# In the tail of a four-image network: new shares for the convolution and the pooled attention of image 2 beside the linear attention of image 3, whose queued steps leave at two of three taps

## The chip, the cores and the metric

The kernel runs on one core of a Trainium2 chip, in one launch. Its time is the device time of a run in microseconds (us); three runs are shown as median, lowest and highest. Beside them one execution was recorded by the hardware profiler: its span reaches from the first to the last instruction. The engines are PE (matrix multiply, with PEld for its weight loads), DVE (vector), ACT (scalar), POOL (GpSimd) and SP (which issues most DMAs).

## The reference

The input x has shape (4, 256, 64, 64), float32. Four layers follow each other, each on a group-normalised x, and each adds its result to x:

```
x = x + L0(gn(x))   # deformable sampling block with a feed-forward part
x = x + L1(gn(x))   # linear attention
x = x + L2(gn(x))   # 3x3 convolution with binarised weights
x = x + L3(gn(x))   # attention over 2x2 max-pooled keys and values
```

What matters here of L1: a 1x1 product gives q, k and v (768 channels); a 5x5 depthwise convolution of these gives a second set; then

```
vk = einsum(v, k); out = einsum(vk, q) / (einsum(k.sum, q) + eps)
out = relu(bn(conv1x1(out)))
```

L3 has 4096 queries and 1024 pooled keys per image: a softmax over the keys, a weighted sum, and a 1x1 product. The four images are independent of each other.

## The kernel before

Images are processed one behind the other, but the layers of different images overlap. Each layer is a generator: it issues some instructions and yields a cost. `beside(steps, number, *works)` in run() interleaves several of them. A work is a tuple (generator, total, lo, hi); while the share i/number goes from lo to hi, the work is advanced whenever the sum of costs that it has yielded is below total * (share - lo) / (hi - lo). From share hi on it is run to its end, and works whose hi is at most 1 are finished before beside returns; one with hi above 1 keeps a remainder. So the totals and shares set only the order in which instructions are issued. Within ordered() that order is what PE, DVE, ACT and POOL execute; each engine takes its instructions in order and waits where data or a buffer isn't ready.

While the sampling of image 3 runs, it is the long work that others lie beside. After it comes the tail, for which run() sets self.alone and self.spare. In the tail there are three parts:

- The first beside: image 3's feed-forward part (share 0 to 0.27), its linear attention layer1 (0.27 to 1, total LAST), and second(2), which is image 2's convolution layer2 followed by its pooled attention layer3 (0.27 to 1.05, total SECOND).
- The second beside: image 3's convolution, with what is left of image 2's pooled attention (total 150).
- Image 3's pooled attention alone.

In layer1 the channels are worked in three rounds of tile pairs, (2, 4), (3, 5) and then the queries (0, 1), each in 4 chunks of 16 image rows. One depthwise convolution of one tile and chunk has 25 taps. In the tail two of three such sets run on DVE (`depthwise`, L178 and L180, 16 sets or 400 taps in all), the third as products on ACT added up on POOL (`products`, L196 and L200). All that follows a finished set, the transposes and outer products (L873 to L882), relu (L861), and the whole output of a chunk, is put as small steps into the list `later`. A step leaves the list from step(), which is called at each tap:

```
if later and (not alone or count % 2 or not chains):
    todo = later.pop(0)
    todo()
```

In the tail (alone is true) this means at every second tap. `output(c, ...)` puts one chunk's output into the list, as 18 steps: the denominators (L924), their reciprocals (L928, L929), eight times a matmul that spreads a reciprocal over its channels (L937) and the product with the queries on DVE (L941), four projections (L946, four matmuls each, two halves of the chunk with two channel tiles each), relu on ACT (L950), the sum with x (L954), its statistics (L110), and the write (L957). There are four such outputs. What is left in the list after the last tap is taken out by a loop at the end, one step per yield of cost 2; this stretch is called the drain.

layer2 holds all its weights in a 3 MB tile (load at L1037), whose pool is opened after the linear attention's pools are closed, for image 3's convolution on the same side of SBUF. It makes the group norm's scale and offset (L117 to L132, with a Sqrt at L98), loads rows (L1050), normalises them (L1051), transforms them on POOL (L1039), multiplies (L1088, 384 matmuls), and sums into x (L1068 to L1072).

layer3 first makes queries, keys and values (L1145 to L1164). Then it takes 32 tiles of 128 queries: scores (L1188, two matmuls), their maximum (L1189, L1190), Exp (L1194), eight transposes (L1200) and two copies (L1202), the weighted sum (L1206, eight matmuls), its reciprocal (L1209) and scale (L1211). After four tiles come a product (L1216), a scale (L1217), a sum (L1218) and the write (L1219). A tile yields costs of 9.5 in all; a whole pooled attention 376.5, a convolution 191, together SECOND = 568.

Of the kernel before, what the change touches and what calls it, by code (L numbers as in the profile page):

```python
# [18 lines left out]
N, C, H, W = 4, 256, 64, 64  # L19
# [19 lines left out]

CONVOLVE, OFFSETS, BINARY = NB * 9 + 26, 60, 62  # L40
FEED = NB * 40 + 8
LINEAR, LAST = 956, 624
STEPS, BEGUN = 900, 0.22
CONV, SECOND = NB * 22.5 + 11, 568
EPS_BN = 1e-5
EPS_GN = 1e-5
# [25 lines left out]
class Net:  # L72
# [684 lines left out]
    def layer1(self, n, st, st2):  # L757
# [3 lines left out]
        with tc.tile_pool(name=f"la{n}", bufs=1, side="right") as sp, \  # L761
# [10 lines left out]
            ld = sp.tile([P, 4, 2, 32], F32, name="ld")  # L772
            nc.vector.memset(ld, 0.0)

            later, count, aside = [], 0, None
            alone = self.alone
            room = lambda bufs, more=1: bufs + more * alone

            def step(cost, chains=False):


                nonlocal count
                count += chains
                if later and (not alone or count % 2 or not chains):
                    todo = later.pop(0)
                    todo()
                    cost += 0 if alone else getattr(todo, "cost", 0)
                if chains:
                    if count % 8 == 6 if alone else count in LEADS:
                        next(made, None)  # L790
                    if count % 2 and aside:
                        next(aside, None)
                return cost
# [51 lines left out]
            def aggregate(pd, i, name, done, relu=True, **more):  # L845

                acc = self.ps1.tile([P, 16, W], F32, name="agg", tag="agg")
                out = bp.tile([P, 16, W], F32, name=name, tag="ag", bufs=3)
                yield from self.depthwise(acc, pd, self.w5[:, i], 5, 16, W, 0, bias=self.b5[:, i:i + 1],
                                          step=lambda cost: step(cost, True), out=out)  # L850
                end(out, done, relu, **more)

            def products(pd, i, name, done, relu=True, **more):

                out = bp.tile([P, 16, W], F32, name=name, tag="av2", bufs=3)
                yield from self.products(bp, out, pd, self.w5[:, i], 5, 16, W, 0, self.b5[:, i:i + 1], lambda cost: cost)
                end(out, done, relu, **more)
# [54 lines left out]

            def output(c, qp, aq):


                qh = [[q[:, 2 + 8 * h:10 + 8 * h, 2:W + 2] for q in qp] + [v[:, 8 * h:8 * h + 8, :] for v in aq] for h in range(2)]
                rd, pd, xv, ot, pb, pr = [], [], [], {}, {}, {}
                spare = cycle(["mm", "vk"])
# [54 lines left out]
            def chains():  # L973

                for _ in range(3 * NCH):
                    while not ready:
                        next(made)
                        yield None
                    t, tiles, c, pd = ready.pop(0)
                    got = {}  # L980

                    def done(i, v, t=t, c=c, pd=pd, got=got):
                        got[i] = v
                        if len(got) < 2:
                            return
                        if t == 2:
                            return output(c, pd, [got[0], got[1]])
                        outer(t, 1, fl(got[0]), fl(got[1]), False, c == NCH - 1)
                        if c == NCH - 1:
                            later.append(partial(summed, t))  # L990

                    for i, m in enumerate(tiles):
                        more = {} if t == 2 or i else {"accum_out": ks[t][:, 1, c:c + 1]}
                        yield pd[i], m, ("ak", "av")[i], partial(done, i), t == 2 or not i, more

            made, number = rows(), 0
            if alone:
                for _ in range(8):
                    next(made)
                    yield step(0.5)  # L1000
                    yield step(0.5)
            every = chains()

            def chain():

                while not (args := next(every)):
                    yield step(3)
                return args

            while number < 6 * NCH:  # L1010
                count = 0 if not alone and number % 2 == 0 else count
                *args, more = yield from chain()
                if alone:

                    *slow, smore = yield from chain()
                    aside = products(*slow, **smore)
                    yield from aggregate(*args, **more)
                    *args, more = yield from chain()
                    yield from aggregate(*args, **more)
                    for _ in aside:  # L1020
                        pass
                    number += 3
                else:
                    yield from aggregate(*args, **more)
                    number += 1
            while later:
                yield step(2 if alone else 1)


    def layer2(self, n, st, st3, side="left"):  # L1030
# [190 lines left out]
    def run(self):  # L1221
# [5 lines left out]
        feed = lambda n: self.feedforward(n, ssum[n], st[1][n % 2])  # L1227
        linear = lambda n: self.layer1(n, st[1][n % 2], st[2][n % 2])

        conv = lambda n, side="left": self.layer2(n, st[2][n % 2], st[3][n % 2], side)  # L1230
        pooled = lambda n, wide=False: self.layer3(n, st[3][n % 2], wide)

        def second(n):
            yield from conv(n)
            yield from pooled(n)

        def beside(steps, number, *works):


            spent, open_ = [0] * len(works), set(range(len(works)))  # L1240

            def advance(share):
                for j in sorted(open_):
                    work, total, lo, hi = works[j]
                    while j in open_ and lo <= share and spent[j] < total * (share - lo) / (hi - lo) or share >= hi:
                        cost = next(work, None)
                        if cost is None:
                            open_.discard(j)
                        if not cost:
                            break  # L1250
                        spent[j] += cost

            for i, _ in enumerate(steps, 1):
                advance(i / number)
            while any(works[j][3] <= 1 for j in open_):
                advance(1)
# [24 lines left out]
                for n in range(2, N):  # L1281
                    beside(self.sample(n, ssum[n]), rounds, *behind(n - 1), (second(n - 2), SECOND, BEGUN, 1))
        self.idle, self.alone, self.spare = cycle(["acc", "dp"]), True, True
        rest = second(N - 2)
        with ordered():
            beside(range(STEPS), STEPS, (feed(N - 1), FEED, 0, 0.27), (linear(N - 1), LAST, 0.27, 1), (rest, SECOND, 0.27, 1.05))
        self.spare = False
        beside(range(STEPS), STEPS, (conv(N - 1, "right"), CONV, 0, 1), (rest, 150, 0, 1))

        self.banks = cycle(["mm", "mm", "mm", "vk"])  # L1290
        for _ in pooled(N - 1, True):
# [95 lines left out]
```

## Time and profile before

| What | us |
| --- | --- |
| Median of three runs | 7640.25 (7638.07 to 7640.4) |
| Profiled execution, its own time | 7631.35 |
| Its span | 7629.6 |
| Busy in the span: PE, DVE, POOL, ACT | 5886.1, 4810.4, 4936.3, 3530.1 |
| Last matmul of the feed-forward part of image 3 | 6401 |
| Last tap of its linear attention | 7131.7 |
| Last projection (L946) | 7208.4 |
| First and last matmul of its convolution | 7238.2, 7417.1 |

A group of the profile is a line of the kernel with engine, operation and tiles, a count, the busy time and the mean of one in ns, then the engine's idle time just before and what ended it. A matmul in float32 stands as two records of one instruction; a transpose as one. The chain of work that ended last names, from the end back, the instruction that each one waited for, or the one before it on its engine. A busy PE is not always PE at its peak, since the ends of matmuls are modelled. PEclk is the clock that PE was granted, as a share of full speed.

### The profile page before, as it was taken

The numbers are of one execution on the slowest core, as the hardware profiler recorded it, in microseconds if no ns is written. First come the engines' busy times: TensorE is split into PE (matmuls) and PEld (weight loads), VectorE is DVE, ScalarE is ACT, GpSimd is POOL, SyncE is SP. The second block draws the span as 40 slices with busy tenths as digits, with TensorE's granted clock in tenths as the row PEclk, the third lists the DMA queues.
The fourth block names the chain that finished last, engine by engine and source line by source line (L and its number), as shares of the span: only waits on it lengthen the run. The fifth ranks groups of instructions, "written<-read, shape, count | busy, mean of one in ns | idle before, by whom it ended". The sixth has DMA issues, their size and how long they took to land. (4 is left out here: it accounts for less than half of the span.)

```text
span 7629.6 us, 99735 instructions
## 1 busy us (share of the span) xinstructions
PE 5886.1 (77%) x35776; PEld 3454.3 (45%) x35776; DVE 4810.4 (63%) x6045; ACT 3530.1 (46%) x10767; POOL 4936.3 (65%) x4870
## 2 busy tenths in 40 slices
PE   5676666678766677888877778988677789967899
PEld 2333333334433333346644443466444445744487
DVE  6454543633688776228988872279888734999623
ACT  2443433444545443445555544454555523655415
POOL 2777777777777777777777676777776702866210
PEclk7676776779877777999988889999888899988999
DMA  6564655565544444555544445455544432210221
GB/s 185 150 188 140 174 170 145 168 185 164 167 124 131 125 141 135 171 150 154 158 147 138 134 138 175 135 168 156 153 133 140 130 103 71 72 53 34 73 81 51
DMA packets 744383, 1031.75 MB, mean 135 GB/s; under 512 B 354128, under 2 KB 459984, under 8 KB 742352
## 3 DMA queue, kind: packets, MB, share of 16 engines
q0 software_dynamic: 221184, 604.27, 27.4%
q1 hardware_dynamic: 522704, 421.10, 18.6%
q8 instruction: 283, 4.64, 0.3%
q14 instruction: 212, 1.74, 0.1%
HBM read 856.39 MB, written 168.61 MB: 134 GB/s over the span
## 5 line engine op out<-in xcount | busy, mean ns | idle before, releaser
L596 POOL DMA_INDIRECT g<-tab,sl x4608 | 4401.1, 955 | 1715.8 <-issue 1271.0
L178 DVE SCALAR_TENSOR_TENSOR agg<-pad,vec,agg 128x1024 f32<-128x1024 f32 x2280 | 2933.7, 1287 | 64.4
L603 PE MATMUL acc<-g,wm 128*32 128x128 f32 x18432 | 1264.0, 321 | 1161.9 <-ACT at L608 670.8
L588 ACT ACTIVATE wm<-sl,con 128x48 f32<-128x48 f32 x6144 | 1487.8, 365 | 23.6 <-DMA sl<-sd 11.9
L603 PEld LDWEIGHTS acc<-g,wm 128*32 128x32 f32 x18432 | 622.1, 121 | 1836.7 <-ACT at L608 888.3
L1088 PE MATMUL ps<-xd,w 128*128 128x256 f32 x3072 | 721.6, 386 | 8.0 <-DVE x L1072 3.5
L1088 PEld LDWEIGHTS ps<-xd,w 128*128 128x128 f32 x3072 | 579.9, 194 | 116.6 <-issue 35.6
L623 ACT COPY dT<-dp 64x128 f32<-64x128 f32 x1152 | 295.5, 256 | 646.4 <-PE dp L613 379.7
L739 PE MATMUL ps<-x2f,f 128*128 128x512 f32 x1024 | 489.8, 625 | 4.0 <-ACT f L714 4.0
L724 DVE SCALAR_TENSOR_TENSOR hm<-ps,vec,lk 128x512 f32<-128x512 f32 x256 | 191.9, 750 | 466.7 <-ACT lk L741 466.2
L824 PE MATMUL ps<-xr,qw 128*128 128x512 f32 x768 | 461.1, 732 | 13.8 <-ACT pT L1202 5.2
L749 PE MATMUL ps<-hm,f 128*128 128x512 f32 x1024 | 468.0, 604 | 0.0
L1039 POOL TENSOR_TENSOR xd<-xp 128x640 f32<-128x640 f32 x64 | 79.6, 1270 | 514.2 <-ACT xp L1051 416.1
L608 ACT COPY at<-acc 128x256 f32<-128x256 f32 x576 | 214.1, 372 | 423.1 <-PE acc L603 411.2
L741 ACT ACTIVATE lk<-ps,low 128x512 f32<-128x512 f32 x256 | 175.9, 687 | 500.5 <-PE ps L739 498.2
L1206 PEld LDWEIGHTS ps<-gt,pT 128*128 128x128 f32 x2048 | 282.6, 216 | 85.9 <-ACT pT L1202 43.4
L1206 PE MATMUL ps<-gt,pT 128*128 128x129 f32 x2048 | 297.6, 304 | 29.8 <-ACT pT L1202 29.1
L613 PE MATMUL dp<-ident,at 128*128 128x128 f32 x1152 | 265.2, 317 | 65.7 <-ACT dT L623 62.9
L636 PE MATMUL po<-dT,ow 128*128 128x288 f32 x1024 | 297.3, 438 | 21.8 <-ACT dT L631 8.9
L1188 PE MATMUL s<-ph,th 128*128 128x512 f32 x512 | 281.6, 663 | 32.9 <-DVE ot L941 11.0
L200 POOL TENSOR_TENSOR ak<-ak,m 128x1024 f32<-128x1024 f32 x96 | 227.6, 2371 | 117.2 <-ACT m L196 112.8
L727 DVE TENSOR_TENSOR xyf<-xyf,ps 128x512 f32<-128x512 f32 x64 | 44.0, 687 | 402.1 <-PE ps L749 389.3
(243 smaller groups left out, 7565.2 us busy)
## 6 DMA issues: line engine op xcount, KB each, us to landing
g<-tab,sl POOLq DMA_INDIRECT x4608
x<-x SPq DMA_DIRECT2D x128, 512.0 KB
xr<-x SPq DMA_DIRECT2D x96, 512.0 KB
tab<-xo SPq DMA_DIRECT2D x192, 128.0 KB
x<-in_x SPq DMA_DIRECT2D x32, 512.0 KB
y<-yc SPq DMA_DIRECT2D x32, 512.0 KB
yb<-y SPq DMA_DIRECT2D x64, 256.0 KB
x<-yb SPq DMA_DIRECT2D x64, 256.0 KB
```

The source lines that it names most:

```text
L178: nc.vector.scalar_tensor_tensor(to, s, wt, acc, ALU.mult, ALU.add)
L588: nc.scalar.activation(wm[:, :, :, o], blocks[b][:, r:r + WR, G:], AF.Copy, scale=self.con("own")[:, o:o + 1])
L596: nc.gpsimd.indirect_dma_start(out=g[:, i, :], out_offset=None, in_=table, in_offset=bass.IndirectOffsetOnAxis(ap=sl.bitcast(I32)[:, r, i: ...
L603: nc.tensor.matmul(acc[32 * i:32 * i + 32, :], wm[:, r4, 4 * i + 2 * x:4 * i + 2 * x + 2, :], g[:, i, x * P:(x + 1) * P], start=x == 0, st ...
L623: nc.scalar.copy(dT[b][hs, :, r:r + UR], dp[u][hs, :, :, s, :].rearrange("p v g o -> p g v o"))
L636: nc.tensor.matmul(po[m][:, 0:BR * OB], self.ow[:, k, m * P:(m + 1) * P], dT[b][:, k].rearrange("p r o -> p (r o)"), start=k == 0, stop=k ...
L739: nc.tensor.matmul(ps, f1[:, k, m * P:(m + 1) * P], x2[:, k], start=k == 0, stop=k == KT - 1)
L749: nc.tensor.matmul(ps, f2[:, k, m * P:(m + 1) * P], hm[:, k], start=k == 0, stop=k == 4 * KT - 1)
L824: nc.tensor.matmul(ps, qw[:, k, m * P:(m + 1) * P], x[:, k], start=k == 0, stop=k == KT - 1)
L1088: nc.tensor.matmul(ps[:, e], w[:, k, t, 2 * half + e, m * P:(m + 1) * P], v[:, 2 * half + e, k, t:t + 8], start=i % 6 == 0, stop=i % 6 == 5)
L1188: nc.tensor.matmul(s[i], tv[:, 4 * b + j], ph[:, i * 512:(i + 1) * 512], start=True, stop=True)
L1206: nc.tensor.matmul(ps[:, 0:P + 1], pT[:, m], gt[:, m], start=m == 0, stop=m == 7)
```

## The change

- layer1 has a new variable `every`, 2 at first, which takes the place of the 2 in `count % 2`. The first call of output() sets it to 3. With 3, `count % every` is zero at every third tap, so steps leave at two of three.
- The loop that empties the list after the last tap yields 1.2 in the place of 2, and the total LAST is 582 in the place of 624.
- Image 2's convolution and pooled attention are two works of the first beside: the convolution with total 191 from share 0.27 to 0.53, the pooled attention with total 376.5 from 0.53 to 1.02. Before, they were one work with total 568 from 0.27 to 1.05.
- In the second beside the rest of the pooled attention has a total of 60 in the place of 150.

The instructions are the same; their order differs. Line numbers in these texts are those of the kernel before.

```diff
-LINEAR, LAST = 956, 624
+LINEAR, LAST = 956, 582
+CONV2, POOLED = 191, 376.5
...
-            later, count, aside = [], 0, None
+            later, count, aside, every = [], 0, None, 2
...
-                if later and (not alone or count % 2 or not chains):
+                if later and (not alone or count % every or not chains):
...
             def output(c, qp, aq):
 
-
+                nonlocal every
+                every = 3
...
-            every = chains()
+            them = chains()
...
-                while not (args := next(every)):
+                while not (args := next(them)):
...
             while later:
-                yield step(2 if alone else 1)
+                yield step(1.2 if alone else 1)
...
-        rest = second(N - 2)
+        rest = pooled(N - 2)
         with ordered():
-            beside(range(STEPS), STEPS, (feed(N - 1), FEED, 0, 0.27), (linear(N - 1), LAST, 0.27, 1), (rest, SECOND, 0.27, 1.05))
+            beside(range(STEPS), STEPS, (feed(N - 1), FEED, 0, 0.27), (linear(N - 1), LAST, 0.27, 1), (conv(N - 2), CONV2, 0.27, 0.53), (rest, POOLED, 0.53, 1.02))
         self.spare = False
-        beside(range(STEPS), STEPS, (conv(N - 1, "right"), CONV, 0, 1), (rest, 150, 0, 1))
+        beside(range(STEPS), STEPS, (conv(N - 1, "right"), CONV, 0, 1), (rest, 60, 0, 1))
```

## The prediction

> **What bounds the kernel now.** I began with the page's slices, to find where the tail starts and which engine fills it.
>
> ```profile
> PE   5676666678766677888877778988677789967899
> DVE  6454543633688776228988872279888734999623
> POOL 2777777777777777777777676777776702866210
> ```
>
> Each digit is 191 us. POOL's first 0 is the slice from 6104 us, after the gathers: what follows is the tail, and the change touches only that. There DVE has its 9s, then PE. The chain that ended last, cut to the tail, gave me the boundaries, and the busy time by stretch gives the table that everything below is summed from.
>
> ```profile
> core 0: us, PE busy (x) PEld busy (x) DVE busy (x) ACT busy (x) POOL busy (x), PEclk, DMA share, GB/s
> 6401.70:6659.30 257.60, 245.13 (x1140) 194.45 (x1140) 223.28 (x295) 155.91 (x221) 201.71 (x101) 0.97 0.30 87
> 6659.30:7131.70 472.40, 330.48 (x1257) 202.69 (x1256) 442.60 (x500) 263.70 (x368) 292.99 (x124) 0.83 0.13 43
> 7131.70:7208.40 76.70, 73.95 (x268) 40.02 (x268) 31.60 (x54) 22.44 (x37) 0.00 (x0) 0.97 0.14 48
> 7208.40:7238.20 29.80, 21.36 (x98) 15.02 (x97) 12.24 (x35) 14.71 (x23) 1.71 (x2) 0.94 0.66 213
> 7238.20:7417.10 178.90, 176.67 (x825) 154.08 (x823) 50.01 (x107) 20.88 (x27) 38.06 (x31) 0.99 0.27 79
> 7417.10:7629.60 212.50, 193.66 (x1040) 145.98 (x1040) 81.34 (x189) 107.33 (x200) 0.00 (x0) 0.97 0.16 55
> ```
>
> The rows are: the taps of image 3's linear attention up to the 140th of 400, beside image 2's convolution; the other 260 taps, beside image 2's pooled attention; the drain (what the linear attention still has queued after its last tap, up to its last projection, L946); the handoff to image 3's convolution; that convolution; image 3's pooled attention alone. DVE sets the pace of the taps (442.6 of 472.4 us), PE that of the drain (73.95 of 76.7) and of the convolution. In the taps PE has 142 us to spare, afterwards nearly none. So a piece moved from behind the last tap to before it costs its DVE time and gives back its PE time.
>
> The DVE durations come from the groups by line of the taps:
>
> ```profile
> L178 DVE SCALAR_TENSOR_TENSOR agg<-pad,vec,agg 128x1024 f32<-128x1024 f32 x368 | 473.0, 1285 | 8.9
> L1189 DVE TENSOR_REDUCE mx<-s 128x1 f32<-128x512 f32 x44 | 28.7, 683 | 5.1 <-PE s L1188 5.0
> ```
>
> A tap costs 1.285 us and waits for almost nothing. What DVE waits for in the second row of the table, from its waits:
>
> ```profile
> DVE mx L1189 <- PE s L1188: 5.0, 9, 1.7
> DVE rden L1209 <- PE ps L1206: 4.2, 3, 2.9
> DVE r L1218 <- PE ps L1216: 3.4, 3, 2.2
> ```
>
> These three are 12.6 us. PE's durations, and what holds the handoff, come from the chain:
>
> ```profile
> 7202.07 6.87 PE ps L946 x16
> 7208.94 1.73 PE s L1188 x4
> 7230.99 1.28 ACT L1194
> 7236.49 4.95 POOL xd L1039 x4
> 7274.97 1.79 PE ps L1206 x16
> 7276.76 5.18 PE ps L1088 x24
> ```
>
> A matmul stands as two records, so a 512-wide one (L946, L1188, L937, L1216) takes 0.86 us, L1206 0.224, a convolution's 0.43; the eight transposes of L1200 are one record each, their loads four in 0.42 us, so 0.107.
>
> **The Trainium skill.** "Perfetto Trace Analysis", Optimization Strategy, says that where the most-contended engine changes over time, interleaving the regimes may gain; the table shows such regimes. "TensorE: Matmul & The Clock Gate", What's actually happening, says that PE's clock halves after an idle window of about 3.4 us and recovers after as long a busy one; the trace agrees: 16 records of L1206 take 3.15 us at 7224.67 in the handoff, 1.79 when warm. "Advanced Engine Details and Errata", Mode Summary, says that VectorE's second SBUF port is shared with GpSimd; the trace fits: L954 takes 1.12 us in the taps, where POOL works, and 0.68 in the drain. "ScalarE: Activation LUTs", What ACT_TABLE_LOAD costs, gives 1.283 us per switch; the trace has 1.28 in the handoff, twice (Sqrt, then Exp), before and after alike.
>
> **The change, part by part.** No instruction is added or removed; I counted by line how many stand ahead of each boundary in the two built programs.
>
> (1) *Pacing.* Per unit of share the linear attention gets 624/0.73 = 855 units before and 582/0.73 = 797 after, the convolution 568/0.78 = 728 and 191/0.26 = 735, the pooled attention 728 and 376.5/0.49 = 768. Against the taps, the convolution runs 8% denser and the pooled attention 13%. 36 units of pooled attention were left for the last overlap, now 15; in the order nothing of it is left among image 3's convolution, which is what the smaller total (60 for 150) then has to place.
>
> (2) *Steps at two of three taps.* From the first output() on, 16.7 steps leave per 25 taps where 12.5 did, so of the last two outputs' 32 projections 24 stay behind the last tap.
>
> Together, ahead of the last tap there are 10 more L1188, 40 L1200, 42 L1206, 2 L1216, 5 L937 and 8 L946. On PE: 8.6 + 4.3 + 9.4 + 1.7 + 4.3 + 6.9 = 35.2 us. On DVE 10 L1189, 5 L1190, 5 L1209, 2 L1218, 6 L941 and 1 L954: 6.9 + 1.1 + 0.8 + 1.4 + 4.1 + 1.1 = 15.4 us.
>
> *Taps.* I summed each engine's work between every 20th tap in both orders, and took the larger of PE and DVE: 703.6 us before, 721.0 after. The 17.4 are the 15.4 and some 2 us more of convolution ahead of the first taps, where PE leads (54.0 to 56.6). Between taps 20 and 140 PE and DVE lie within 2 us of each other per 20 taps, and the denser convolution passes DVE nowhere there: that is its cover, and if PE's work were 5% dearer it would pass DVE in three of the six, by 4 us in all. Really the taps took 730.0, 26.4 above the sum, in waits. DVE's reads of PE results after the convolution grow from 94 to 117; at 12.6/94 = 0.13 us each, 3 us more. Taps: +20.5 us. POOL's halvings for the convolution (L1039) pass some of its additions, with POOL at 202 of 258 us, nothing added; on SP's queue one 512 KB load and one output move past the last tap, at a DMA share of 0.13, nothing.
>
> *Drain.* PE's work there: 32 L946 27.5, 14 L937 12.0, 10 L1188 8.6, 40 L1200 4.3, 42 L1206 9.4, 8 L924 1.9, 2 L1216 1.7, sum 65.4 us in 76.7. After: 20.6 + 7.7 + 5.2 + 2.6 + 3.6 + 1.9 + 1.7 = 43.3, at the same ratio 50.8. Drain: -25.9; between -19 (the 11 us of slack grow to 14, or so) and -28.
>
> *Handoff.* Not PE's: the last projection, its relu, sum and statistics, then the group norm's two small matmuls, Sqrt, Exp's table again, the normalised rows (L1051) and POOL's first halving. In it PE's in-order pooled pieces stand between (L120 only ran at 7223.0, behind transposes that waited for an Exp). Pooled work there falls from 8 L1188 and 24 L1200 to 4 and 16, one of its tile chains fewer, some 5 us of 29.8. The 3 MB of w2, asked for at 7216.0, didn't end a wait before and starts no later. Handoff: -5, between -8 and +1.
>
> *Convolution.* Its 383 remaining matmuls are 165.3 us; 2 L1188, 16 L1200, 16 L1206 and 2 L1216 (8.7 us) leave it, and with them stalls: 178.9 - 174.0 = 4.9 us, where PE waited for copies queued on ACT behind rows that were still loading. Without these I leave 1 us of stall. Against that PE comes from an emptier handoff, so 3.4 us at half clock, 1.7 us. Sum -8.7 - 3.9 + 1.7 = -11; between -8 and -13.
>
> *The end* has the same instructions in both: 0.
>
> Sum: 20.5 - 25.9 - 5 - 11 = -21.4 us. Against the profiled run's own 7631.35 us (span 7629.6) that is 7610; the median of the runs is 8.9 us above that run, and the same step from it, 7640.25, gives 7619.
>
> **Rivals.** (A) *DVE waits for a fuller PE.* Steps that leave at neighbouring taps give PE 1.29 us, where two taps gave 2.6, between a matmul such as L937 and the L941 that reads it. If a read waits 0.26 us instead of 0.13, 117 reads cost 15 more: 7634. For it: PE's granted clock was only 0.83 in the taps, and single waits reached 2.9 us. Against: no L941 waited there before, and PE keeps a quarter of its time free. (B) *The drain is a chain of latencies*, not PE's work: it falls by 8, not 26, us: 7637. For it: reciprocal, relu and sum follow each other; against: PE was busy 73.95 of 76.7. (C) *Slower*: rival A's mechanism at its worst, PE as bound of the output's taps. At 0.5 us a read, 117 x 0.37 = 43 us more: 7662. It decides from 0.13 + 21.4/117 = 0.31 us a read. Against: the largest bin after has PE at 30.2 and DVE at 42.3 us. (D) *More than forecast*: +17, -28, -8, -13: -32, 7608. That the steps don't move is excluded by the order.
>
> **How the numbers follow.** Forecast 0.58, A 0.17, B 0.09, C 0.08, D 0.08. The likeliest gives 7619, its own range 7611 to 7627. The range of 8 in 10 takes in D's side to 7604 and A and B to 7639; C is left out, with some of D's. Under 0.2% (15.3 us) a measurement of this kernel can't tell a change from none, so 7625 is the border: D, and all but a tenth of the forecast, lie below it, 0.68 with a part kept for misjudged terms; within 0.2% A, B and the rest, 0.24; slower 0.08.
>
> **What would show it.** The last tap (L178) ends near 7152 instead of 7131.7; the drain lasts some 51 us, the handoff 25, the convolution 168, with records of L1088 alone in it; the last stretch stays at 212. It is wrong if DVE's waits for PE in the taps pass 30 us, if PE's share of the drain drops below 80%, or if the handoff grows because PE and w2 come late to it.

## The result and the profile after

The changed kernel takes 7607.24 us (median of six runs, 7600.57 to 7611.53); the kernel before, on the same chip, 7640.03 (six runs, 7638.07 to 7641.73). The ratio is 0.9958, with a 95% interval of 0.9947 to 0.9968: faster by 0.42%. The forecast was 7619, its range 7604 to 7639.

The profiled execution of the changed kernel took 7611.53 us, its span is 7609.7. In `L` numbers of its profile one is added up to L914 and two beyond (L178 is L179, L946 is L948, L1088 is L1090); in this document the numbers in the text stay those of the kernel before, unless a shown line has the other.

First the busy tenths in 40 slices of the page of after, in the same three rows:

```profile
PE   5676666578766677888877778888777789977899
DVE  6454543633688877228988872279988833999723
POOL 2777777777777777777777676777777711865320
```

The shape is that of before; in the tail PE differs by one digit, a 7 for a 6 in the 36th slice (6658 to 6849 us), which lies in the taps. By stretch of the tail, with the boundaries taken in the same way (last matmul of the feed-forward part, 140th tap, last tap, last projection, first and last matmul of the convolution), after's busy times are:

```profile
core 0: us, PE busy (x) PEld busy (x) DVE busy (x) ACT busy (x) POOL busy (x), PEclk, DMA share, GB/s
6408.60:6672.30 263.70, 253.50 (x1194) 204.46 (x1194) 225.55 (x300) 155.96 (x221) 198.91 (x100) 0.97 0.29 85
6672.30:7162.10 489.80, 358.28 (x1387) 225.76 (x1386) 452.22 (x524) 279.53 (x397) 297.16 (x125) 0.84 0.13 43
7162.10:7210.10 48.00, 45.56 (x157) 22.79 (x156) 23.78 (x39) 16.77 (x26) 0.00 (x0) 1.00 0.22 77
7210.10:7230.70 20.60, 14.32 (x81) 10.21 (x79) 9.19 (x31) 11.25 (x17) 1.31 (x2) 1.00 0.77 259
7230.70:7397.20 166.50, 166.26 (x768) 145.75 (x768) 45.62 (x96) 14.08 (x15) 38.25 (x31) 1.00 0.29 85
7397.20:7609.70 212.50, 193.96 (x1040) 145.97 (x1040) 81.44 (x189) 107.30 (x200) 0.00 (x0) 0.97 0.16 55
```

The convolution is bare now: 768 records are its 384 matmuls and nothing else, and PE is busy in 166.26 of 166.5 us. Against the table of before, in us:

| | head | taps | drain | handoff | convolution | end | tail |
| --- | --- | --- | --- | --- | --- | --- | --- |
| before | 6401.8 | 729.9 | 77.2 | 29.3 | 178.8 | 212.5 | 1227.7 |
| after | 6408.6 | 753.5 | 48.0 | 20.6 | 166.5 | 212.5 | 1201.1 |
| difference | +6.8 | +23.6 | -29.2 | -8.7 | -12.3 | 0.0 | -26.6 |
| forecast | 0 | +20.5 | -25.9 | -5 | -11 | 0 | -21.4 |

In this table the drain ends with the end of the last projection, 0.5 us later than in the prediction's rows: hence 77.2 and 29.3 for its 76.7 and 29.8. The head is all that comes ahead of the last feed-forward matmul, and the change doesn't touch it. It was 6400.5 to 6408.6 us in six profiled executions at this level of time, of kernels that don't differ in it. The kernel before's profiled execution (7631.35 us) lies below all six of its runs given above, and that of after is the longest of its own; so the two profiles differ by 19.8 us and the medians by 32.8. The tail accounts for 26.6. The other 6 us are not seen in any stage that the change touches.

Two views of the taps. DVE's groups by line in the taps of after:

```profile
L179 DVE SCALAR_TENSOR_TENSOR agg<-pad,vec,agg 128x1024 f32<-128x1024 f32 x368 | 472.9, 1285 | 8.6
L1191 DVE TENSOR_REDUCE mx<-s 128x1 f32<-128x512 f32 x54 | 35.6, 685 | 3.6 <-PE s L1190 3.3
```

A tap costs what it did (1285 ns), and there are ten more maxima, 54 for 44. And DVE's waits from the 140th tap on (us in total, times, longest):

```profile
DVE rden L1211 <- PE ps L1208: 8.0, 5, 2.6
DVE r L1220 <- PE ps L1218: 5.5, 4, 2.1
DVE mx L1191 <- PE s L1190: 3.3, 13, 0.8
```

The same three waits were 12.6 us before and are 16.8 now. Over all the taps DVE is busy 709.9 us for 695.7, and idle 43.6 for 34.2. Busy is here, and wherever DVE's busy and idle time are compared below, the sum of its instructions' durations, and idle the rest. Neighbouring instructions overlap by some 30 us in all, which the table by stretch counts once: there DVE is busy 677.8 us for 665.9, and has nothing running for 75.7 us, where before had 64.0.

What leads from the last projection to the convolution, by the chain of work that ended last (start, duration, what):

```profile
7206.67 3.45 PE ps L948 x8
7210.14 0.79 ACT pr L952
7210.95 0.70 DVE xq L956
7211.67 3.06 DMA x<-xq
7215.69 6.89 SPq L1052
7222.62 6.74 DMA x<-x
7229.39 4.95 POOL xd L1041 x4
```

Before, the chain went through Exp's table (L1194) there. Now no pooled work stands in it: relu, sum and write of the last projection, then SP, then the rows. The group norm's scale and offset were ready 12.6 us after the last projection, the rows only after 19.2. SP's timeline (start, time to issue), before and then after:

```profile
7216.01 0.34 SPq L1037 DMA_DIRECT2D w<-w  x1
7219.27 0.38 SPq L1219 DMA_DIRECT2D out<-r  x1
7219.69 1.16 SPq L1050 DMA_DIRECT2D xp<-x  x2
```

```profile
7214.82 0.34 SPq L1039 DMA_DIRECT2D w<-w  x1
7215.22 7.36 SPq L1052 DMA_DIRECT2D xp<-x  x2
```

In after the two row loads stand directly behind the 3 MB of w2 and took 7.36 us to issue, where they took 1.16 before. With what landing then takes, the first rows are there 14.5 us after w2 was asked for.

### The profile page after: what moved, and what is told of

Same layout as the page of the kernel before. It is cut to its first block, busy times and chain, and to the rows that moved or that the text cites. A ratio compares the mean times of both kernels' runs of the same rounds, so it can differ in the third digit from the quotient of the medians.

```text
span 7609.7 us, 99719 instructions
## 1 busy us (share of the span) xinstructions
PE 5883.1 (77%) x35776; PEld 3453.7 (45%) x35776; DVE 4806.8 (63%) x6045; ACT 3533.9 (46%) x10767; POOL 4952.2 (65%) x4870
## 5 line engine op out<-in xcount | busy, mean ns | idle before, releaser
L179 DVE SCALAR_TENSOR_TENSOR agg<-pad,vec,agg 128x1024 f32<-128x1024 f32 x2280 | 2934.1, 1287 | 64.1
L1090 PE MATMUL ps<-xd,w 128*128 128x256 f32 x3072 | 714.5, 385 | 9.1 <-POOL xd L1041 5.9
L1090 PEld LDWEIGHTS ps<-xd,w 128*128 128x128 f32 x3072 | 578.2, 193 | 113.1 <-issue 29.4
L1190 PE MATMUL s<-ph,th 128*128 128x512 f32 x512 | 281.1, 662 | 32.9 <-DVE ot L943 11.1
L201 POOL TENSOR_TENSOR av<-av,m 128x1024 f32<-128x1024 f32 x96 | 228.0, 2375 | 112.7 <-ACT m L197 108.6
```

The costliest lines, as they stand in the source:

```text
L179: nc.vector.scalar_tensor_tensor(to, s, wt, acc, ALU.mult, ALU.add)
L201: nc.gpsimd.tensor_tensor(acc, acc, made[t - 1], ALU.add)
L1090: nc.tensor.matmul(ps[:, e], w[:, k, t, 2 * half + e, m * P:(m + 1) * P], v[:, 2 * half + e, k, t:t + 8], start=i % 6 == 0, stop=i % 6 == 5)
L1190: nc.tensor.matmul(s[i], tv[:, 4 * b + j], ph[:, i * 512:(i + 1) * 512], start=True, stop=True)
```

## The experiments

Theory 1 is the prediction's: a piece moved ahead of the last tap costs its DVE time there and gives back its PE time behind it. Rival 1 says that one half of the change alone carries the gain. Rival 2 is the prediction's A: reads of a fuller PE make DVE wait. A theory 3 was formed after the first four runs. The first four and four later ones ran where the kernel before takes about 8740 us: there POOL waits 2824.0 us ahead of its gathers (L596) for 1715.8, with the same 4395.5 us of gathering for 4401.1, while the tail is 1225.1 us for 1227.7. The first four were on another chip, but the four later ones bear the number of the chip of the shorter times, so what makes these two levels of time isn't known. Ratios are taken within a level, and stages of the tail across both. The changed kernel's stages repeated within 0.3 us (after again, below), those of before within 1.9 and its tail within 2.6, across the two levels. In the versions made from after, some statements are joined on one line, so that their line numbers are those of before.

### The halves: the steps alone

The kernel before with the steps at two of three taps, LAST and the loop's 1.2; the works and their shares stay.

```diff
-LINEAR, LAST = 956, 624
+LINEAR, LAST = 956, 582
...
-                if later and (not alone or count % 2 or not chains):
+                if later and (not alone or count % every or not chains):
...
+                nonlocal every; every = 3
...
-                yield step(2 if alone else 1)
+                yield step(1.2 if alone else 1)
```

> The steps alone: from the first output on two of three taps, 1.2 per step in the loop after the last tap and a total of 582 for the linear attention; the pooled attention and the convolution of image 2 stay one work with a total of 568, and 150 in the second overlap. By theory 1 (each piece that moves from behind the last tap to before it costs its DVE time there and gives back its PE time): taps 747 us (sum of the larger engine 716.4, and some 30 of waits), drain 49 (PE work 42.5), handoff 24, convolution 179 as before (174.0 of PE work with the rest of image 2's pooled attention in it): 999 against 1015 before, so about 16 us faster. By rival 1 (the gain is the cleared convolution and handoff, and faster steps only trade DVE time for drain time): 5 us or less.

Measured: 8720.66 us, ratio 0.9977 (0.9968 to 0.9986). Tail 1218.7, so -9.0. Its drain and its convolution, by stretch, in the columns of the table of after:

```profile
8253.70:8301.30 47.60, 44.52 (x153) 21.86 (x152) 22.73 (x37) 13.74 (x22) 0.00 (x0) 1.00 0.16 56
...
8324.50:8504.10 179.60, 176.52 (x824) 154.23 (x824) 49.98 (x104) 20.75 (x27) 38.67 (x31) 0.99 0.27 79
```

The drain has all of after's gain (47.6, -29.6), the convolution none (179.6, +0.8). The taps grew by 26.1, to 756.0 us where theory 1 had 747: the 9.0 us lie between its 16 and the 5 of rival 1.

### The halves: the works alone

The kernel before with image 2's two works apart, and after's shares and remainder; steps leave at every second tap.

```diff
-        rest = second(N - 2)
+        rest = pooled(N - 2)
...
-            beside(..., (rest, SECOND, 0.27, 1.05))
+            beside(..., (conv(N - 2), 191, 0.27, 0.53), (rest, 376.5, 0.53, 1.02))
...
-        beside(range(STEPS), STEPS, (conv(N - 1, "right"), CONV, 0, 1), (rest, 150, 0, 1))
+        beside(range(STEPS), STEPS, (conv(N - 1, "right"), CONV, 0, 1), (rest, 60, 0, 1))
```

> The split alone: convolution and pooled attention of image 2 as two works with 191 and 376.5, and 60 in the second overlap; steps at every second tap, 2 per step after the last tap and 624 as before. Theory 1: taps 734 us (sum 706.9), drain 79 (PE work 68.9), handoff 25, convolution 167 (only its own 165.3): 1005 against 1015, so about 11 us faster. Rival 1: 25 us or more, most of the whole change's 33.

Measured: 8735.53 us, ratio 0.9993 (0.9986 to 1.0). Tail 1225.4, -2.3. The same two stretches:

```profile
8251.70:8331.40 79.70, 77.10 (x275) 41.32 (x274) 33.10 (x56) 25.76 (x43) 0.00 (x0) 0.95 0.18 60
...
8358.10:8524.80 166.70, 166.26 (x768) 145.75 (x768) 46.26 (x99) 14.08 (x15) 38.26 (x31) 1.00 0.29 84
```

Now the convolution has the gain (-12.2) and the drain none (+2.4); the taps grew by 11.1, to 741.0 us where theory 1 had 734, and of its 11 us 2.3 are left. Against before again, which ran at the level of these two, the tails are -6.4 (the steps) and +0.3 us (the works). Rival 1 falls, for its 25 us and more aren't there: the drain belongs to the steps and the convolution to the works, and behind the last tap the two add up (drain -27.2 for -29.2, handoff -8.7 for -8.7, convolution -11.4 for -12.3).

In the taps they don't:

| against before, us | taps | DVE busy | DVE idle | tail |
| --- | --- | --- | --- | --- |
| steps alone | +26.1 | +14.4 | +11.7 | -9.0 |
| works alone | +11.1 | -1.3 | +12.4 | -2.3 |
| their sum | +37.2 | +13.1 | +24.1 | -11.3 |
| after | +23.6 | +14.2 | +9.4 | -26.6 |

DVE's work adds up to 1 us, its waits are 15 short. This split isn't sharp: before again has 691.2 us busy and 38.7 idle with the same instructions, for 695.7 and 34.2. The length of the taps doesn't hang on it: together they cost 13.6 us less than the sum. The sums of work explain the drain and the convolution; these 13.6 us they don't explain.

### A step at every tap

After, with the outputs' steps leaving at every tap:

```diff
-                nonlocal every
-                every = 3
+                nonlocal every; every = 99999
```

> The whole change, but from the first output on a step leaves at every tap. Only 16 projections are left behind the last tap. Theory 1: taps 761 us (sum 728.4), drain 35 (PE work 31.0), handoff 22, convolution 167: 985, 3 us under the changed kernel's 988. Rival 2 (DVE comes to wait for PE where steps leave at neighbouring taps): DVE's waits in the taps grow by 15 us or more over the changed kernel's, and the time is 12 us above it.

Measured: 8748.48 us, ratio 1.0004 (0.9996 to 1.0012). Tail 1228.7, 27.6 above after's. Taps 782.6 (+29.1), drain 39.7, handoff 28.5, convolution 166.0. DVE was busy 715.0 us in the taps, 5.1 more than in after, and idle 67.6, 24.0 more. DVE's waits there from 7789.5 us on (us in total, times, longest):

```profile
DVE mx L1189 <- PE s L1188: 13.9, 15, 5.5
DVE rden L1209 <- PE ps L1206: 12.6, 8, 3.9
```

Theory 1 misses (it had 3 us less than after) and rival 2's mechanism holds. These two waits are 15.2 us longer than in after: mostly the pooled pieces find PE occupied. The outputs' own pieces add 8.9 (L954 waits 5.1 us for ACT, L941 once 3.1 for PE, L928 0.7 more). The handoff of 28.5 us is set by three tiles of pooled attention one behind the other; the chain of work that ended last has this of one of them, ahead of the convolution:

```profile
8356.57 1.83 PE s L1188 x4
8358.42 0.70 DVE mx L1189
8359.39 0.69 ACT pe L1194
8360.13 1.24 PE pt L1200 x8
8361.61 1.97 PE ps L1206 x16
```

With three engines in turn a tile takes 7 to 10 us there, and PE waits for the Exp in each. The rows, issued from 8354.93 on in 6.80 us, end no wait in this run.

### The pooled attention earlier

After, with the pooled attention finished within the taps:

```diff
-(rest, POOLED, 0.53, 1.02))
+(rest, POOLED, 0.53, 0.97))
```

> The whole change, but image 2's pooled attention ends at share 0.97 and not 1.02, so that all of it stands ahead of the last projection, and the handoff has no pooled work in it. Theory 1: taps 762 us (sum 729.2), drain 42 (PE work 37.3), convolution 167; the handoff, with nothing of PE in it, shows what the path of the group norm and of the loads costs by itself: 18 to 20 us if that path is the bound, as I think; under 12 if the pooled pieces in PE's order had held it up. Sum 989 to 991, within 3 us of the changed kernel.

Measured: 8758.42 us, ratio 1.0021 (1.0015 to 1.0028). Tail 1249.0, 47.9 above after's, and 50.6 of it in the taps (804.1), with 44.6 more of DVE's idle time (88.2) and 6.0 more of its work. DVE's waits from 7771.4 us on, in the same columns:

```profile
DVE mx L1189 <- PE s L1188: 27.7, 22, 4.8
DVE rden L1209 <- PE ps L1206: 20.2, 14, 3.0
```

In all of DVE's gaps over 0.15 us in this stretch, whatever ended them, PE was busy 69.1 of 72.6 us (in after, in the same stretch, 26.5 of 29.5). So PE isn't waiting too: it is working on what DVE needs or on something that stands ahead of it in its order. Theory 1's sum (within 3 us of after) misses. That PE has over a quarter of the taps to spare (in after 131.5 of 489.8 us) covers nothing at these places.

The handoff, 19.8 us, within the expected 18 to 20, has almost no PE work (1.18 us), so it shows the path of the loads without PE's pieces; of the chain of work that ended last (start, duration, what):

```profile
8362.20 6.29 SPq L1050
...
8368.53 6.54 DMA x<-x
```

The same two waits as in after, at 6.3 and 6.5 us. After's handoff of 20.6 is within 1 us of this.

### Four tiles back, and after again

Some four tiles of the pooled attention returned to image 3's convolution, against the changed kernel run again on the same chip:

```diff
-(rest, POOLED, 0.53, 1.02))
+(rest, POOLED, 0.53, 1.10))
-(rest, 60, 0, 1))
+(rest, 270, 0, 1))
```

> The changed kernel again (the same program, two statements joined to one line so that line numbers are those of before). If the stretch up to the last feed-forward matmul, which the change does not touch, differs only by chance, the stages after it are those of the first profile within 1 us each (taps 753.5, drain 48.0, handoff 20.6, convolution 166.5, end 212.5), and the time is about 27 us under that of the kernel before. If that stretch is shorter in the changed program itself, the time is 33 us under.

> The whole change, but the pooled attention of image 2 is spread to share 1.10 and not 1.02 (total 270 for its rest), so that some four tiles of it go back from the taps to the convolution of image 3. Theory 1: taps 745 us (sum 713.0 and 32 of waits), drain 44 (PE work 39.4), handoff 22, convolution 193 (PE work 187.8 and stalls as before the change): 1004, some 15 above the changed kernel's 988.6, since each of these tiles then costs its 5 us of PE and saves 2 us of DVE. Theory 3, formed after the first experiments (DVE's waits for PE grow faster than the work that is moved, so that the changed kernel is near the best point): the taps fall by more than 8.5, to under 742, and the sum is within 10 us of the changed kernel's.

Measured: after again 7605.55 us, ratio 0.9959 (0.9946 to 0.9973), tail 1201.4. Its stages repeat, but the time is 32.7 us under the median of before and not 27, and its head of 6402.4 isn't shorter than the 6401.8 of before's profile: this doesn't settle the 6 us. Four tiles back 7627.09, ratio 0.9986 (0.998 to 0.9993), tail 1223.6, so 22.2 above after again. Its convolution, by stretch:

```profile
7221.50:7415.10 193.60, 190.50 (x902) 164.60 (x902) 56.63 (x118) 26.57 (x38) 38.38 (x31) 0.99 0.26 78
```

The convolution grew by 27.2 us, 24.2 of it PE's work; the taps shrank by only 7.7 (745.9), 9.1 less of DVE's work. This is theory 1's exchange with the sign reversed, somewhat dearer than it expected; theory 3's numbers fall. With the run before it, the remainder has been moved to either side of the changed kernel's: both sides are slower, at 0.97 by the waits in the taps and at 1.10 by PE's work in the convolution.

### The rows ahead of w2

After, with the first rows of image 3's convolution loaded ahead of w2, to see whether the handoff hangs on them:

```diff
-            nc.sync.dma_start(w, self.w2_d)
-            sc, bi = yield from self.groupnorm(sp, st, "g2")
+            def rows(b):
...
+            early = [rows(0)] if side == "right" else []
+            nc.sync.dma_start(w, self.w2_d)
+            sc, bi = yield from self.groupnorm(sp, st, "g2")
...
+                xp, vs = early.pop() if early else rows(b)
```

> The whole change, and in image 3's convolution the first rows are loaded ahead of the 3 MB of w2, not behind them. In the changed kernel's profile these rows' small packets come only after the last of w2. If the load queue is the bound of the handoff, it falls from 20.6 us by 2 to 4 us, to what w2 itself takes (asked for at 4.7 us after the last projection, some 9 to 11 us long) or the scale and offset of the group norm (ready 12.5 us after it) with the 5 us of ACT and POOL behind them; if the path of the norm is the bound, it stays within 1 us. Other stages as in the changed kernel.

Measured: 7604.63 us, ratio 0.9958 (0.9944 to 0.9972); the handoff is 22.0, 1.4 above after's. The loads did what was meant, by SP's timeline of this kernel (here the row loads are L1047, w2 is L1051):

```profile
7206.72 1.02 SPq L1047 DMA_DIRECT2D xp<-x  x2
7207.78 1.21 SPq L1051 DMA_DIRECT2D w<-w  x1
```

The rows were issued in 1.02 us, and POOL's first transform of them (L1039 in before) ran 14.5 us after the last projection, for 19.3 in after. But PE's timeline (L1214 is the weighted sum, L1224 the pooled product), and DVE's below it:

```profile
7217.56 3.59 PE L1214 MATMUL ps<-gt,pT 128*128 128x129 f32 x16
7222.15 1.99 PE L1224 MATMUL ps<-m,ww 128*128 128x512 f32 x4 [1.00 <-ACT m L1219]
```

```profile
7221.55 0.07 DVE L1044 MEMSET xp<- 128x20 f32 x1 [6.92 <-POOL xd L1053]
7221.56 0.14 DVE L1217 RECIPROCAL rden<-ps 128x1 f32<-128x1 f32 x1
```

The last pooled tile now stands in the way, in PE's order, at half clock (3.59 us for 16 records that take 1.79 warm; the granted clock was 0.5 from 7217.45 to 7220.86). DVE's reciprocal for it stood behind a border memset of the next rows, which waited 6.92 us for POOL to be done with the buffer, but only the last 0.4 us of that delayed it, since the weighted sum ended at 7221.15. The expectation (2 to 4 us less) missed, and it could hardly have been met: in after PE was done with its last pooled product at 7229.06, only 1.65 us before it began the convolution, so that without the loads the handoff had 1.65 us to gain, in the same order. That the loads come last in after is read from its chain and from the run without pooled work; this run, in which another wait took their place, doesn't show it by their removal.

### The same change at slightly other shares

Since the taps of both halves together are 13.6 us shorter than their sum, the waits may hang on how pieces happen to fall between the taps. After with its shares moved by 0.005 and 0.0025, and before with its shares moved by 0.005 and -0.002, with no other difference:

```diff
-(conv(N - 2), CONV2, 0.27, 0.53), (rest, POOLED, 0.53, 1.02))
+(conv(N - 2), CONV2, 0.27, 0.53), (rest, POOLED, 0.535, 1.025))
```

The second shift of after has 0.5325 and 1.0225; those of before have `(rest, SECOND, 0.275, 1.055)` and `(rest, SECOND, 0.268, 1.048)`. The kernel before itself was also run once more beside the last three.

> The whole change, but the pooled attention of image 2 starts and ends 0.005 later (0.535 to 1.025): the same work stands ahead of the last tap but for 3 transposes and 8 of L1206, only set elsewhere between the taps. If DVE's waits for PE follow from how much is moved, the taps stay within 2 us of 753.5; if they follow from where the pieces fall between the taps, they change by 5 us or more either way while DVE's busy time stays at 710.

> The whole change, with the pooled attention of image 2 set 0.0025 of share later (0.5325 to 1.0225), half the shift of the experiment before, and the same work ahead of the last tap but for 3 of L1206. If the place decides, the tail lies anywhere between 1201 and 1225; with the two profiles at 1201 and 1222 it shows whether 1201 is a usual value or a favourable one.

> The kernel before, with the convolution and pooled attention of image 2 set 0.005 of share later (0.275 to 1.055). The work ahead of the last tap is nearly the same (8 transposes and 6 of L1206 less, one L937 more). If the place of the pieces between the taps decides DVE's waits as much as their number, the tail moves by 5 us or more from 1227.7, either way; if only their number counts, it stays within 3 us.

> The kernel before, with the convolution and pooled attention of image 2 set 0.002 of share earlier (0.268 to 1.048). The same question with a smaller shift and nearly the same work ahead of the last tap (5 of L1206 less): 5 us or more from 1227.7 if the place decides, within 3 us if the number does.

> The kernel before, profiled again. Its tail repeats within 1 us (1227.7 from the last feed-forward matmul to the end). Open is the stretch ahead of it: 6401.8 us in the first profile, whose time was 9 us under the median of the runs. If that profile was a short one by chance, the stretch is 6408 to 6412 here, as the medians say; if it is 6402 again, the medians' 6 us of gain beyond the tail stay unexplained.

Measured (one execution each; us from the stages of the profile):

| | taps | drain | handoff | convolution | tail | DVE idle in the taps |
| --- | --- | --- | --- | --- | --- | --- |
| after / again | 753.5 / 753.6 | 48.0 / 48.0 | 20.6 / 20.7 | 166.5 / 166.4 | 1201.1 / 1201.4 | 43.6 / 43.4 |
| after, +0.0025 | 755.2 | 53.5 | 23.7 | 166.2 | 1210.8 | 45.9 |
| after, +0.005 | 764.7 | 53.7 | 25.8 | 166.0 | 1222.3 | 54.8 |
| before / again | 729.9 / 730.0 | 77.2 / 77.2 | 29.3 / 29.3 | 178.8 / 176.9 | 1227.7 / 1225.1 | 34.2 / 38.7 |
| before, +0.005 | 727.2 | 81.6 | 31.1 | 180.6 | 1232.4 | 31.5 |
| before, -0.002 | 740.7 | 84.6 | 24.5 | 174.8 | 1236.9 | 44.5 |

The totals were 7625.03 for after +0.005 (beside a median of 7638.22 for before at its level), and 8716.56, 8739.96, 8742.84 and, for before again, 8736.61 at the other.

So the place decides: after +0.005 has 11.2 us more of taps with DVE busy 710.0 us as in after. For before, -0.002 is 9.2 us above 1227.7; +0.005 is 4.7 above it, just under the 5 us that were asked for, and 7.3 above before again, which ran at its level. Before again's tail repeated within 2.6 us and not 1, and its head of 7509.7 us, at the other level, doesn't bear on the 6 us.

What a single wait looks like in after +0.005, by PE's timeline and then DVE's (line numbers as in before):

```profile
7149.54 3.75 PE L1206 MATMUL ps<-gt,pT 128*128 128x129 f32 x16
7153.13 3.60 PE L946 MATMUL ps<-ot,pw 128*128 128x512 f32 x8
7156.65 1.12 PE L937 MATMUL rden<-rd,con 64*128 64x512 f32 x2
7157.71 2.09 PE L1188 MATMUL s<-ph,th 128*128 128x512 f32 x4
```

```profile
7153.41 1.27 DVE L178 SCALAR_TENSOR_TENSOR agg<-pad,vec,agg 128x1024 f32<-128x1024 f32 x1
7159.05 1.48 DVE L1189 TENSOR_REDUCE mx<-s 128x1 f32<-128x512 f32 x2 [4.36 <-PE s L1188]
```

After the tap DVE came to a maximum at 7154.7 and stood for 4.36 us, with more taps behind it in its order; the scores that it waited for stood on PE behind a weighted sum at half clock, a projection and a spread, 8.2 us of work between 7149.54 and 7157.71. The clock is part of it: what "TensorE: Matmul & The Clock Gate" of the Trainium skill says under What's actually happening, that the clock halves after an idle window, agrees as to the halving: the granted clock was 0.5 from 7142.9 to 7153.1, and the 16 records took 3.75 us for 1.79 warm. PE's longest idle stretch just before was 3.16 us; no run here shows how long one has to be.

Such a shift changes no instruction, only where a few of them stand. It moves the tail by 9.5 and 21.0 us with the new shares, by 6.0 and 10.5 with the old. Of the 21.0, 11.1 lie in the taps, all of it DVE's idle time, and 10.8 in drain and handoff; of the 9.5 nearly all (8.5) lies in these two. There PE's clock differs. Drain and handoff of after +0.005, in the columns of the table of after:

```profile
7165.70:7219.40 53.70, 49.42 (x164) 24.04 (x163) 24.15 (x38) 15.60 (x25) 0.00 (x0) 0.94 0.20 69
7219.40:7245.20 25.80, 19.84 (x88) 14.31 (x86) 8.44 (x30) 11.80 (x19) 1.32 (x2) 0.80 0.62 206
```

After had 1.00 in both; after +0.0025 has 0.94 and 0.86. If PE works throughout, a granted clock of 0.94 loses 6% of the stretch, so an estimate from these columns is 0.06 x 53.7 + 0.20 x 25.8 = 8.4 of the 10.8 us, and 6.5 of the 8.5 for +0.0025. Whether the idle stretches of PE or the low clock that followed them cost more wasn't separated.

Over the three placements of each, with the repeated kernels at the mean of their two profiles, the tails average (1201.3 + 1210.8 + 1222.3)/3 = 1211.5 and (1226.4 + 1232.4 + 1236.9)/3 = 1231.9: 20.4 us apart. Three placements are few, and they are of both levels; but the forecast of 21.4 is that of a change at a typical placement, and the placement that the change has is better than the other two tried. That part of its gain is luck.

## Why the prediction was right

The time, 7607.24, lies in the range, 12 us below the forecast and 4 outside the likeliest case's own range of 7611 to 7627; it is nearly rival D's 7608, in which all the stages come out at or near their better ends. It got there in another way: the taps were worse than forecast, and the three stages behind them better by 8.3 us together. By the steps:

- **Taps**, +20.5 forecast, +23.6 measured. DVE's work, 15.4 forecast, was +14.2. Waits, 5 us of the forecast (2 of PE's lead ahead of the first taps and 3 of DVE's reads), were +9.4. That is less than rival A's 15, though A's mechanism is real: the step at every tap and the earlier pooled attention pay it with 24 and 45 us. The three waits that the forecast had priced at 0.13 us a read came to 16.8 us for 117 reads, 0.14 each. What it had not priced is a wait for the denominators (L928, 2.8 us) and longer waits of DVE among image 2's convolution, where its waits for PE went from 14.1 to 16.9 us. Nor is the price a constant: it depends on where PE's pieces stand, and the shift of 0.005 alone made 11 us more. The prediction's own sign of being wrong, more than 30 us of DVE's waits for PE in the taps, could not tell: counted over all the taps these waits (gaps over 0.15 us) were 32.1 us before and are 41.2 after.
- **Drain**, -25.9 forecast, -29.2 measured, just past the better end of its bounds. The count of PE's work was good; the term that was mis-sized is the ratio of 76.7/65.4. The stretch took 48.0 us for the 43.3 counted, a factor of 1.11 for 1.17. Most of this is the clock: PEclk was 0.97 in the drain before and 1.00 after, by the estimate used above 0.03 x 76.7 = 2.3 of the 2.8 us by which 48.0 lies under the forecast 50.8 (the other 0.5 of the 3.3 is the boundary). Rival B, a chain of latencies, is excluded by 45.56 us busy of 48.0 and by the steps alone, which had the same drain.
- **Handoff**, -5 forecast, -8.7 measured, just past its better end; the path named was wrong. The forecast kept the group norm behind PE's pooled pieces and let w2 end no wait. In after the loads end it: the rows behind w2 on SP (7.36 us to issue) come last, and the run without pooled work there took 19.8 us. That w2 was free before didn't mean that it stayed free once the rest was shorter, and the text had asked what is late next only for PE. Here too PE's clock went from 0.94 to 1.00. The two loads of ACT's function tables (1.28 us each, for Sqrt and for Exp) are in both handoffs, as the prediction had it.
- **Convolution**, -11 forecast, -12.3 measured. The terms of work and stalls, 8.7 and 3.9 us, make 12.6 together. The 1.7 us of half clock that were set against them didn't come: PEclk was 1.00 in both the handoff and the convolution, and in the handoff PE did 14.32 us of work in 20.6. And the stall left was 0.24 us for the 1 us allowed. Some of the 12.3 is chance in the kernel before: its convolution took 178.8 us at a clock of 0.99 in the first profile and 176.9 at 1.00 in the second.
- **The end**, 0 forecast, 0.0 measured.
- **The base.** -26.6 of the tail from the median of before, 7640.03, gives 7613.4; the median is 7607.24. The 6 us between are of the head, or of executions that weren't profiled, and stay open. They are also in other comparisons: the steps alone gained 9.0 us in the tail of their profile, and by the ratio some 20 us of their time; the four tiles back 4.1 and some 11. Median less tail, and less the 1.8 us by which a time exceeds its span, leaves a head of 6409 to 6411 us for before and of 6401 to 6404 for the four kernels with several runs and the new shares at its level. The mechanism says nothing of this, so 6 of the 32.8 us are not explained by it.
- **The chances.** The 0.68 for a time under 7625 is more than the prediction's own chances give: 0.08 for D and nine tenths of 0.58 make 0.60.

So the sign comes from the mechanism named: the 50.2 us that the three stages behind the last tap lost were bought with 23.6 us of taps. The halves show each term at its place. The size is owed in part to the placement: the two halves alone brought 9.0 and 2.3 us where this reasoning expected 16 and 11, and the whole brought more than the sum. How much of the gain is left depends on the waits and on PE's clock, which no sum of work over 20 taps contains. In the end better stages behind the last tap made up for worse taps. Why just this placement waits less than its neighbours wasn't traced beyond single gaps. The rows ahead of w2, the one version that went beyond the change, came out the same: 7604.63 beside 7605.55 for after again.

## What to carry to other kernels

Where the engine that sets the pace changes from stage to stage, price each moved piece by the old stage's pacing engine and the new one's, as here by DVE's 15 us and PE's 35 us; that holds to a few us per stage. Waits between in-order engines are not in such sums: before trusting the last 10 us, run the same order shifted by a fraction of a step, and take the spread (here 6 to 21 us) as the uncertainty of any fine placement. Look at the granted clock of each stage before giving a difference of a few us to the work in it. When a handoff shrinks, list every load in it with its issue time and its landing, also those that ended no wait before, and what PE itself still has to do there.

## What the hardware showed beyond that

- A row load issued directly behind the 3 MB load of w2 took 6.9 us to issue in after and 6.3 in the run with the earlier pooled attention; with the rows first, both rows took 1.02 us and w2 1.21. Before, 3.3 us after w2 was issued and behind a write, both rows took 1.16 us.
- In DVE's gaps over 0.15 us PE is busy 87 to 97% of the time, in either part of the taps (up to the 140th, and from there on), in thirteen of the profiles, though after has a quarter of PE free from the 140th tap on: the two engines are rarely both idle.
- The sum with x (L954) takes 1.22 us on the mean in the taps of after and 0.70 in its handoff, on the same shape. The mean hides two cases: 1.41 to 1.84 us in the five executions that began while an addition ran on POOL, 0.68 or 0.69 in the other four. The product with the queries (L941), of the same shape, took 0.67 or 0.68 us in all twelve that began while POOL was adding. L954 has both its inputs in SBUF, L941 one of them in PSUM. This agrees with "Advanced Engine Details and Errata" of the Trainium skill, Mode Summary, that VectorE's second SBUF port is shared with GpSimd.
